# Attention and ternary FFN on one core: the FFN's middle layer laid out with its channels on partitions

## The chip, the cores and the metric

The kernel runs on one core of a Trainium2 chip. Its engines work side by side, each through its own queue in order: TensorE (PE, with its weight loads as PEld), VectorE (DVE), ScalarE (ACT), GpSimd (POOL) and SyncE (SP, which here only starts DMAs). The metric is the device time of one execution, in microseconds; lower is better. The kernel before takes 735.78 us (median of three runs, 735.1 to 738.06).

## The reference

The input x is 8 x 1024 x 256 in float32. First comes a linear attention with 16 heads of 16, its own LayerNorm and an output projection, added to x, and a LayerNorm. Then comes a feed-forward network, added to its input, and a last LayerNorm:

```python
h = layer_norm(x, ln1_g, ln1_b)
h = jnp.einsum('bsd,hd->bsh', h, ternary_quant(w1)) + b1     # 256 -> 1024
h = jax.nn.gelu(h, approximate=False)
h = layer_norm(h, ln2_g, ln2_b)                              # over the 1024
out = jnp.einsum('bsh,dh->bsd', h, ternary_quant(w2)) + b2   # 1024 -> 256
```

`ternary_quant` turns a weight matrix into -1, 0 and 1 times one scale. The middle layer is what lies between the two products: bias, gelu, and a LayerNorm over its 1024 channels.

## The kernel before

The 8192 rows are 16 blocks of 512 rows (`blocks`), a block being four tiles (`G`) of 128 rows; x stays in SBUF (`xs`) all the time and takes the results in place. The program is written out by hand in one order (`manual_schedule`), and each engine gets its instructions in that order. The main loop runs 18 times (`i`): for i up to 15 it makes the keys, queries and state of block i, and it does `attend` for block i - 2. Small DVE work of the attention's LayerNorms waits in the lists `soon` and `later` and is dealt out a few steps at a time by `more(n)`; the normalised rows are written by ACT through `apply(n)`. The weights' quantisation (`prepare1`, `prepare2`) is dealt out the same way, by `next(prep)`.

The FFN is a generator, `ffn_slots`, of one slot for each of 128 chunks (16 blocks times 8). Its slots are drawn 13 times in the last two turns of the main loop (`slot()`, i = 16 and 17), where the last two blocks are attended, and then one after the other to the end, with `more(8)` and `apply(2)` after each. In the code:

- `enter` (L571): POOL multiplies a block's rows by a scale into `h0` (L576), and a POOL DMA adds the row `bout` onto x (L579).
- `turn_input` (L583): PE turns `h0`, ACT and DVE split it into two fp32r halves `hT`, high and low (`halves`, L568 on ACT and L569 on DVE). A value goes through the fp32r products as these two halves.
- `hidden` (L597), once a slot: 128 rows by 512 channels. The rows are the stationary operand and `t1` moves: four products of 512 columns (L615), and a fifth of a row of ones with the row `brow`, which adds the bias (L619). ACT applies Gelu and sums along the row (L620).
- `squares` (L629), every second slot: ACT squares the deviation from the mean over 1024 channels, with the sum taken along (L632).
- `turn` (L636), once a slot: four transposes bring 128 channels of the block's 512 rows onto partitions (L643), then the halves `u`, scaled by ln2's gain (L568, L569).
- `product` (L648), once a slot: eight products of 256 columns (L657) add the chunk to the outputs `pf` of four row tiles, which sit two to a PSUM bank.
- `norms` and `outputs`, in fixed slots of a block: DVE computes the two inverse roots with integer steps and three Newton steps (`rsqrt`, L122 to L131), adds the mean term (`add_mean`, L680), adds the product out of PSUM to x (L716), takes statistics (L686, L687); `finish` (L663) lets POOL write the last LayerNorm (L670) and SP store the block (L673).

A slot s works on `product(s)`, `turn(s + 2)` and `hidden(s + 11)`: `hidden` runs 11 slots ahead.

Of the kernel before, what the change touches and what calls it, by code (L numbers as in the profile page):

```python
# [22 lines left out]
def attn_ffn_postln_kernel(  # L23
# [29 lines left out]


# [4 lines left out]
    t2 = const.tile([P, HC, C], F32R, name="t2")  # L59
# [6 lines left out]
    bkv = const.tile([P, 2 * KC], F32, name="bkv")  # L66
    nc.sync.dma_start(xs[0][:, 0:G, :], x0[:, 0:G, :])
    nc.scalar.dma_start(wqkv_sb[:, :, C : 2 * C], w3[:, :, C : 2 * C])
    with nc.allow_non_contiguous_dma("two vectors of 256"):
        nc.gpsimd.dma_start(bkv, rows[C : 3 * C].rearrange("(i p) -> p i", p=P))  # L70
# [9 lines left out]
    )  # L80
    for b in range(1, B):
        nc.sync.dma_start(xs[b], x[b].rearrange("(p t) c -> p t c", p=P))
# [10 lines left out]
    nc.vector.memset(ones, 1.0)  # L93

# [42 lines left out]
    brow = const.tile([P, HID], F32R, name="brow")  # L137
    ones_r = const.tile([P, P], F32R, name="ones_r")
    g2sum = const.tile([P, C], F32, name="g2sum")
    bout = const.tile([P, C], F32, name="bout")  # L140
    nc.vector.memset(ones_r.bitcast(F32), 1.0)
# [3 lines left out]
    def quantise(w, t_sb, inv, name):  # L145
        t_all = t_sb.rearrange("p a b -> p (a b)")
        n = t_all.shape[1]
        o = min(w.shape[1], 512)

        def pieces(what):  # L150

            for k in range(w.shape[0] // P):
                for c in range(0, w.shape[1], o):
                    piece = big.tile([P, TB], F32, tag="hA", bufs=4, name=f"{what}_{name}_{k}_{c}")
                    nc.sync.dma_start(piece[:, :o], w[k * P : (k + 1) * P, c : c + o])
                    yield k * w.shape[1] + c, piece[:, :o]
# [10 lines left out]
        for i, piece in ahead(pieces("wm")):  # L167
            yield
            nc.vector.tensor_reduce(
                part[:, i // o : i // o + 1], piece, AX.X, ALU.add, apply_absolute_value=True  # L170
            )
# [4 lines left out]
        total = ps.tile([P, TB], F32, tag="tp", bufs=2, name=f"total_{name}")  # L176
# [6 lines left out]
        for i, piece in ahead(pieces("wq")):  # L183
            yield
            nc.vector.tensor_scalar(piece, piece, scale, 1.0, ALU.mult, ALU.min)
            nc.vector.tensor_scalar(piece, piece, -1.0, ROUND, ALU.max, ALU.add)
            nc.vector.tensor_scalar(t_all[:, i : i + o], piece, ROUND, None, ALU.subtract)

    def spread(made, cols, vec, name):

        if not made:
            made.append(big.tile([P, HC, P], F32, tag="h0", bufs=2, name=f"col_{name}"))
        for j in cols:
            nc.vector.tensor_scalar(made[0][:, j, :], ones, vec[:, j : j + 1], None, ALU.mult)
        return made[0]

    def prepare1():
# [4 lines left out]
        sel = const.tile([P, 1], F32, name="sel")  # L202
        nc.vector.tensor_tensor(sel, ident[:, 0:1], ident[:, 1:2], ALU.subtract)
        for j in range(0, HID, 512):
            yield
            b1_b = big.tile([P, TB], F32, tag="hA", bufs=4, name=f"b1_{j}")
            nc.sync.dma_start(
                b1_b, rows[5 * C + j : 5 * C + j + TB].partition_broadcast(P)
            )
            col = spread([], range(KC), ln1_b, f"1_{j}")  # L210
            yield
            pb = ps.tile([P, TB], F32, tag="tp", bufs=2, name=f"pb_{j}")
            for k in range(KC):
                nc.tensor.matmul(
                    pb, col[:, k, :], t1[:, k, j : j + 512].bitcast(F32),
                    start=(k == 0), stop=(k == KC - 1),
                )
            full = b1_b
            nc.vector.scalar_tensor_tensor(full, pb, inv1, b1_b, ALU.mult, ALU.add)
            yield  # L220
            hi = big.tile([P, TB], F32R, tag="hA", bufs=4, name=f"hi_{j}")
            nc.vector.tensor_copy(hi, full)

            nc.vector.tensor_scalar(full, full, ident[:, 1:2], None, ALU.mult)
            nc.vector.scalar_tensor_tensor(
                brow[:, j : j + 512], hi.bitcast(F32), sel, full, ALU.mult, ALU.add
            )

    def prepare2():

        yield from quantise(w2, t2, inv2, "w2")
        for i, vec in enumerate((ln2_g, ln2_b)):
            made = []
            for j in range(0, HC, 2):
                yield
                col = spread(made, (j, j + 1), vec, f"2_{i}")
            yield
            pg = ps.tile([P, TB], F32, tag="tp", bufs=2, name=f"ps2_{i}")
            for j in range(HC):
                nc.tensor.matmul(  # L240
                    pg[:, 0:C], col[:, j, :], t2[:, j, :].bitcast(F32),
                    start=(j == 0), stop=(j == HC - 1),
                )
            if i == 0:
                nc.vector.tensor_copy(g2sum, pg[:, 0:C])
            else:
                nc.vector.scalar_tensor_tensor(bout, pg[:, 0:C], inv2, b2_b, ALU.mult, ALU.add)
# [11 lines left out]
    def prepare0():  # L259
        yield  # L260
        col = spread([], range(KC), ln_b, "0")
        pc = ps.tile([P, TB], F32, tag="tp", bufs=2, name="ps_crow")
        for k in range(KC):
            nc.tensor.matmul(
                pc[:, 0:C], col[:, k, :], wo_sb[:, k, :], start=(k == 0), stop=(k == KC - 1)
            )
        nc.vector.tensor_tensor(crow, pc[:, 0:C], bo_b, ALU.add)
        yield
        pm = ps.tile([P, TB], F32, tag="tp", bufs=2, name="ps_mean")
# [27 lines left out]
    def turned(dst, src, k, name):  # L297

        pt = ps.tile([P, TB], F32, tag="tp", bufs=2, name=name)
# [44 lines left out]
    def turn_keys(i, t):  # L344
# [3 lines left out]
        pt = ps.tile([P, TB], F32, tag="tp", bufs=2, name=f"pte_{i}_{t}")  # L348
# [97 lines left out]
    def state_turn(b):  # L446
        pt = ps.tile([P, TB], F32, tag="tp", bufs=2, name=f"pta_{b}")
# [9 lines left out]
    def state_values(b):  # L457

        pst = ps.tile([P, TB], F32, tag="tp", bufs=2, name=f"pst_{b}")
# [14 lines left out]
    def state_out(b, c):  # L474
# [3 lines left out]
        pm = ps.tile([P, TB], F32, tag="tp", bufs=2, name=f"psm_{b}_{c}")  # L478
# [7 lines left out]
    def attend(i, t):  # L486
# [6 lines left out]
        if t == 0:  # L493
            ys[i] = big.tile([P, G, C], F32, tag="y", bufs=5, name=f"y_{i}")
# [7 lines left out]
        o = big.tile([P, KC, P], F32, tag="o", bufs=4, name=f"o_{i}_{t}")  # L502
# [59 lines left out]
    SLOTS = len(blocks) * HC  # L562
    LEAD = HC + 3
    h0, hT, h, u, pf, mv, rs, sc, ms = {}, {}, {}, {}, {}, {}, {}, {}, {}

    def halves(hi, lo, src, gain):

        nc.scalar.activation(hi, src, AF.Copy, scale=gain)  # L568
        nc.vector.scalar_tensor_tensor(lo, src, gain, hi.bitcast(F32), ALU.mult, ALU.subtract)  # L569
# [13 lines left out]
    def turn_input(i, k):  # L583
        if k == 0:
            tag, bufs = ("xT", 2) if i % 2 == 0 else ("qT", 3)
            hT[i] = [
                big.tile([P, KC, TB], F32R, tag=tag, bufs=bufs, name=f"hT_{i}_{s}")
                for s in range(2)
            ]
        pt = ps.tile([P, TB], F32, tag="tp", bufs=2, name=f"pth_{i}_{k}")  # L590
# [4 lines left out]
        halves(hT[i][0][:, k, :], hT[i][1][:, k, :], pt, gs1[:, k : k + 1])  # L595

    def hidden(m):  # L597


        i, t, half = m // HC, m % HC // 2, m % 2  # L600
        if half == 0:
            if t == 0:
                h[i] = []

                mv[i] = small.tile([P, 2 * G, 2], F32, tag="mvh", name=f"mvh_{i}")
                if i == 0:
                    nc.vector.memset(mv[i][:, :G, :], 1.0)
            tag, bufs = ("hA", 4) if i % 2 == 0 else ("y", 5)
            h[i].append(big.tile([P, HID], F32, tag=tag, bufs=bufs, name=f"h_{i}_{t}"))
            h[i, t] = small.tile([P, 2], F32, tag="total", name=f"total_{i}_{t}")  # L610
        cols_j = slice(half * 512, (half + 1) * 512)
        ph = ps.tile([P, TB], F32, tag="w", bufs=4, name=f"ph_{m}")
        for s in range(2):
            for k in range(KC):
                nc.tensor.matmul(  # L615
                    ph, hT[i][s][:, k, t * P : (t + 1) * P], t1[:, k, cols_j],
                    start=(s == 0 and k == 0), stop=False,
                )
        nc.tensor.matmul(ph, ones_r, brow[:, cols_j], start=False, stop=True)  # L619
        nc.scalar.activation(  # L620
            h[i][t][:, cols_j], ph, AF.Gelu, accum_out=h[i, t][:, half : half + 1]
        )
        if half == 1:
            nc.vector.tensor_scalar(  # L624
                mv[i][:, G + t, 0:1], h[i, t][:, 0:1], h[i, t][:, 1:2], -1.0 / HID,
                ALU.add, ALU.mult,
            )

    def squares(i, t):  # L629

        sq = big.tile([P, HID], F32, tag="sq", name=f"sq_{i}_{t}")
        nc.scalar.activation(  # L632
            sq, h[i][t], AF.Square, bias=mv[i][:, G + t, 0:1], accum_out=mv[i][:, G + t, 1:2]
        )

    def turn(s):  # L636

        i, j = s // HC, s % HC
        tag, bufs = (("q", 2), ("ekT", 1), ("q", 2), ("ek", 1))[s % 4]
        u[s] = big.tile([P, 2, TB], F32R, tag=tag, bufs=bufs, name=f"u_{s}")  # L640
# [275 lines left out]
```

## Time and profile before

| what | value |
|---|---|
| three runs, median | 735.78 us |
| the profiled execution, its own time | 737.86 us |
| its span, first to last instruction | 736.2 us |
| mean granted TensorE clock | 0.981 |
| busy PE / PEld / DVE / ACT / POOL | 690.2 / 548.9 / 556.3 / 441.6 / 177.0 us |
| first `hidden` product (L615) starts | 351.5 us |
| first `product` (L657) starts | 379.9 us |
| last `product` starts | 723.9 us |
| last store is issued | 732.6 us |

The span has three parts: attention to about 351 us, a mixture of the last two attended blocks and the first FFN slots to 380 us, and FFN alone from there. A row of a group of instructions gives line, engine, operation, output and inputs with their shapes, how often, total busy time, the mean of one, then the engine's idle time just before them and what ended it. A row of the timeline gives start, duration, engine, line, operation and how many like it are merged. The duration of one instruction holds its latency, and instructions of one engine overlap (eight L657 of 0.28 us each span 1.20 us in the timeline), so what an engine spends on each is read from the distance between two starts.

### The profile page before, as it was taken

Reading aid. Unit: us, or ns where it says so; the run is one execution under the profiler, and the core shown is the slowest. Engines: PE = TensorE matmul, PEld = TensorE weight load, DVE = VectorE, ACT = ScalarE, POOL = GpSimd, SP = SyncE. Lnnn points to the kernel's source line nnn. Section 1 sums busy time; section 2 is a strip of 40 time slices with the busy share of each in tenths; the row PEclk is TensorE's granted clock in tenths of the full one; section 3 lists DMA queues with packets and bytes.
Section 4 is the critical chain, followed back from the end, with each engine's and each line's share of the span. In section 5 each row is a group of like instructions: output and inputs, shape, how many; then the busy total and the mean of one; then the engine's idle time right before and its main releaser. Section 6 shows DMA issues by size and latency. Waiting matters only on the chain.

```text
span 736.2 us, 10803 instructions
## 1 busy us (share of the span) xinstructions
PE 690.2 (94%) x3780; PEld 548.9 (75%) x3780; DVE 556.3 (76%) x1642; ACT 441.6 (60%) x970; POOL 177.0 (24%) x156
## 2 busy tenths in 40 slices
PE   6899999979989999997998899999999999999992
PEld 4677766757657777765776788888888888888882
DVE  1567799886997859797888766767766777776686
ACT  2245445635464545646797677677677677776760
POOL 1222213121221212224310023333113333113112
PEclk9999999998999999999999999999999999999998
DMA  9832203222011211203510022220122220222001
GB/s 329 292 86 48 40 15 65 51 44 51 8 30 28 30 29 18 40 1 57 87 29 1 1 58 58 58 57 31 29 58 58 58 57 30 30 57 58 30 30 58
DMA packets 25687, 40.43 MB, mean 55 GB/s; under 512 B 1600, under 2 KB 21056, under 8 KB 24736
## 3 DMA queue, kind: packets, MB, share of 16 engines
q0 software_dynamic: 17056, 17.17, 15.8%
q1 hardware_dynamic: 7344, 21.50, 7.8%
q10 hardware_dynamic: 1232, 1.06, 0.4%
q8 instruction: 30, 0.49, 0.3%
q14 instruction: 25, 0.20, 0.1%
HBM read 14.56 MB, written 8.39 MB: 31 GB/s over the span
## 4 chain that ended last, share of the span: by engine, by line
PE 63%; DVE 19%; issue 9%; ACT 4%; DMA 3%; POOL 2%; ACTq 0%; POOLq 0%; DVEq 0%
PE ph L615 12%; PE pf L657 12%; PE po L498 7%; PE pt L643 5%; PE pa L407 5%; PE pq L364 5%; PE pk L322 5%; PE ph L619 3%; DMA wo_sb<-in_wo_dram 3%; DVE x L526 2%; DVE st_y L532 2%; POOL x L670 2%; PE ptq L301 1%; PE pth L592 1%; PE ptx L301 1%
## 5 line engine op out<-in xcount | busy, mean ns | idle before, releaser
L657 PE MATMUL pf<-t,u 128*128 128x256 f32 x1024 | 156.8, 294 | 4.0 <-DVE x L716 3.6
L569 DVE SCALAR_TENSOR_TENSOR u<-pt,cols_sb,u 128x512 fp32r<-128x512 f32 x128 | 95.6, 747 | 66.0 <-ACT u L568 64.3
L615 PE MATMUL ph<-t,hT 128*128 128x512 f32 x512 | 143.7, 402 | 0.0
L657 PEld LDWEIGHTS pf<-t,u 128*128 128x128 f32 x1024 | 131.0, 189 | 10.0 <-issue 5.8
L620 ACT ACTIVATE h<-ph 128x512 f32<-128x512 f32 x128 | 76.6, 598 | 84.6 <-PE ph L619 74.3
L670 POOL TENSOR_SCALAR x<-x,ny_f,sh 128x256 f32<-128x256 f32 x60 | 38.5, 652 | 270.9 <-DVE sh L667 270.9
L615 PEld LDWEIGHTS ph<-t,hT 128*128 128x128 f32 x512 | 88.7, 189 | 13.6
L498 PE MATMUL po<-sm,qT 128*128 128x384 f32 x256 | 96.6, 502 | 0.0
L568 ACT ACTIVATE u<-pt,cols_sb 128x512 fp32r<-128x512 f32 x128 | 87.5, 684 | 8.4 <-PE pt L643 8.4
L643 PE MATMUL pt<-ident,h 128*128 128x128 f32 x512 | 77.8, 274 | 4.7 <-DVE u L569 2.6
L643 PEld LDWEIGHTS pt<-ident,h 128*128 128x128 f32 x512 | 61.3, 140 | 21.2 <-DVE hT L569 7.0
L632 ACT ACTIVATE sq<-h,mvh 128x1024 f32<-128x1024 f32 x64 | 73.8, 1153 | 1.9 <-DVE mvh L624 1.9
L378 POOL TENSOR_TENSOR q<-q,qm 128x1024 f32<-128x1024 f32 x16 | 30.8, 1926 | 149.8 <-DVE qm L377 90.5
L407 PE MATMUL pa<-x,ek 128*128 128x256 f32 x256 | 63.2, 392 | 0.0
L364 PE MATMUL pq<-wqkv_sb,xT 128*128 128x256 f32 x256 | 60.6, 380 | 1.0 <-DMA wqkv_sb<-in_wqkv_dram 1.0
L322 PE MATMUL pk<-xT,wqkv_sb 128*128 128x512 f32 x128 | 60.9, 599 | 0.0
L407 PEld LDWEIGHTS pa<-x,ek 128*128 128x128 f32 x256 | 50.5, 198 | 13.5 <-issue 0.6
L498 PEld LDWEIGHTS po<-sm,qT 128*128 128x128 f32 x256 | 45.8, 195 | 18.8 <-issue 1.7
L364 PEld LDWEIGHTS pq<-wqkv_sb,xT 128*128 128x128 f32 x256 | 47.9, 190 | 12.8 <-issue 3.1
L391 POOL TENSOR_TENSOR q<-q,rq 128x1024 f32<-128x1024 f32 x16 | 31.0, 1935 | 108.8 <-DVE rq L390 63.1
L338 ACT ACTIVATE ekT<-pk,nb 128x512 f32<-128x512 f32 x32 | 21.7, 683 | 55.3 <-DVE nb L335 29.5
L619 PE MATMUL ph<-brow,ones_r 128*128 128x512 f32 x128 | 50.7, 396 | 0.0
(144 smaller groups left out, 1109.9 us busy)
## 6 DMA issues: line engine op xcount, KB each, us to landing
x<-crow POOLq DMA_DIRECT2D x16, 512.0 KB, 5.5
x<-bout POOLq DMA_DIRECT2D x16, 512.0 KB, 5.5
out_dram<-x SPq DMA_DIRECT2D x16, 512.0 KB, 2.6
x<-in_x_dram SPq DMA_DIRECT2D x7, 1024.0 KB, 9.8
x<-in_x_dram SPq DMA_DIRECT2D x2, 512.0 KB, 5.8
wm_w<-in_w_dram SPq DMA_DIRECT2D x4, 256.0 KB, 4.0
wq_w<-in_w_dram SPq DMA_DIRECT2D x4, 256.0 KB, 2.5
wm_w<-in_w_dram SPq DMA_DIRECT2D x8, 128.0 KB, 2.1
```

Source lines behind the costliest of these rows:

```text
L322: nc.tensor.matmul(pk, wqkv_sb[:, k, C + c * P : C + (c + 1) * P], xT[i][:, k, :], start=(k == 0), stop=(k == KC - 1),)
L364: nc.tensor.matmul(pq[:, n, :], xT[i][:, k, (t + n) * P : (t + n + 1) * P], wqkv_sb[:, k, 0:C], start=(k == 0), stop=(k == KC - 1),)
L407: nc.tensor.matmul(pa[i][:, c, :], ek[i][:, t, c * P : (c + 1) * P], x_of(i)[:, t, :], start=(t == 0), stop=(t == G - 1),)
L498: nc.tensor.matmul(po[:, c * P : c * P + P + C], qT[i][:, c, t * P : (t + 1) * P], sm[b][:, c, :], start=(c == 0), stop=(c == KC - 1), ski ...
L568: nc.scalar.activation(hi, src, AF.Copy, scale=gain)
L569: nc.vector.scalar_tensor_tensor(lo, src, gain, hi.bitcast(F32), ALU.mult, ALU.subtract)
L615: nc.tensor.matmul(ph, hT[i][s][:, k, t * P : (t + 1) * P], t1[:, k, cols_j], start=(s == 0 and k == 0), stop=False,)
L619: nc.tensor.matmul(ph, ones_r, brow[:, cols_j], start=False, stop=True)
L620: nc.scalar.activation(h[i][t][:, cols_j], ph, AF.Gelu, accum_out=h[i, t][:, half : half + 1])
L632: nc.scalar.activation(sq, h[i][t], AF.Square, bias=mv[i][:, G + t, 0:1], accum_out=mv[i][:, G + t, 1:2])
L643: nc.tensor.transpose(pt[:, t * P : (t + 1) * P], h[i][t][:, j * P : (j + 1) * P], ident)
L657: nc.tensor.matmul(pf[i][t // 2][:, t % 2, :], u[s][:, n, t * P : (t + 1) * P], t2[:, j, :], start=(j == 0 and t % 2 == 0 and n == 0), sto ...
```

## The change

The middle layer is made with channels on partitions. A chunk is now 128 channels by the block's 512 rows. `hidden` takes `t1` as the stationary operand and moves `hT`: four products of 512 columns into a bank `ph`. The bias is a column now, so Gelu takes it as its per-partition operand (`bh`), in place in PSUM. ACT copies `ph` to the high half of `u`, scaled by `gm`, and squares `ph` about a constant `shift` into `sq`; DVE makes the low half (`lower`). The transposes of `turn`, the bias products, the row sums and `spread` are gone.

The sum of squares over channels is now a sum over partitions: POOL adds the eight `sq` of a block into `sums` (seven adds of 128 x 512), and four small products with a column of ones (`sum_squares`) make it a number per row. The row sums of h come from two more columns of `t2` (258 instead of 256), which hold the high and low half of 1/`gm`; `gm` is the gain's mantissa, and its power of two goes into `t2`. `shift` is minus the mean of gelu(bias) over all channels; `scales` corrects the variance for it.

`pf` is one bank for each of the four row tiles (tag `w`); at a block's end ACT copies them to SBUF (`take`, into `z`), and DVE's `output` reads `z`. `ph` rotates through three banks (two of tag `o`, one `tq`), `u` through nine buffers (`RING`). The inverse root of the FFN's scales (`power`) is a POOL power with one Newton step; the two other roots keep `rsqrt`.

The order of a block is the string `ORDER`: P is a product, H a `hidden` with its ACT work, r a portion (`R`) of the previous block's closing DVE work (`rest`), e an `enter`, a and b the two `turn_input`, s `sum_squares`. H runs seven to eight chunks ahead of P. In this stage `more` deals one step every second unit and `apply` one every eighth; in the turns 16 and 17 of the main loop they are cut to two and one. `prep` ends one turn earlier, and the first `enter` and `turn_input` go into turns 13 and 14. Some attention buffers shrink (`y` from 5 to 4, `o` from 4 to 3), the PSUM tag `tp` becomes two tags in turn, and the bias comes by one more POOL DMA at the start.

```diff
...
-    t2 = const.tile([P, HC, C], F32R, name="t2")
+
+    t2 = const.tile([P, HC, C + 2], F32R, name="t2")
...
+    with nc.allow_non_contiguous_dma("vectors of 512 and 1024"):
+        nc.gpsimd.dma_start(b1, rows[5 * C :].rearrange("(i p) -> p i", p=P))
...
+        yield
+        pb = ps.tile([P, TB], F32, tag=next(turning), bufs=1, name="pb1")
+        for j in range(HC):
             for k in range(KC):
                 nc.tensor.matmul(
-                    pb, col[:, k, :], t1[:, k, j : j + 512].bitcast(F32),
-                    start=(k == 0), stop=(k == KC - 1),
+                    pb[:, j : j + 1], t1[:, k, j * P : (j + 1) * P].bitcast(F32),
+                    ln1_b[:, k : k + 1], start=(j == 0 and k == 0),
+                    stop=(j == HC - 1 and k == KC - 1), skip_group_check=True,
                 )
+        nc.vector.scalar_tensor_tensor(bh, pb[:, 0:HC], inv1, b1, ALU.mult, ALU.add)
...
+        yield
+        gb = cols_sb[:, 8:24].rearrange("p (v j) -> p v j", v=2)
+        pg = yield from rows_of(
+            lambda j: t2[:, j, :C].bitcast(F32), lambda j: gb[:, :, j], HC, "2"
+        )
+        nc.vector.tensor_copy(g2sum, pg[:, 0, :])
+        nc.vector.scalar_tensor_tensor(bout, pg[:, 1, :], inv2, b2_b, ALU.mult, ALU.add)
+        yield
...
+        nc.vector.tensor_scalar(
+            gm.bitcast(I32), ln2_g.bitcast(I32), 0x7FFFFF, 0x3F800000,
+            ALU.bitwise_and, ALU.bitwise_or,
+        )
...
+        nc.vector.reciprocal(inv, gm)
+        nc.vector.tensor_copy(t2[:, :, C], inv)
+        nc.vector.tensor_tensor(t2[:, :, C + 1], inv, t2[:, :, C].bitcast(F32), ALU.subtract)
+        for j in range(HC):
...
+            nc.vector.tensor_scalar(
+                t2[:, j, :C], t2[:, j, :C].bitcast(F32), power[:, j : j + 1], None, ALU.mult
+            )
...
-            ys[i] = big.tile([P, G, C], F32, tag="y", bufs=5, name=f"y_{i}")
+            ys[i] = big.tile([P, G, C], F32, tag="y", bufs=4, name=f"y_{i}")
...
-        o = big.tile([P, KC, P], F32, tag="o", bufs=4, name=f"o_{i}_{t}")
+        o = big.tile([P, KC, P], F32, tag="o", bufs=3, name=f"o_{i}_{t}")
...
+    WEIGHT = 8
+    ORDER = "ePHaPHPrHrPbHPrHrPrHrsPrHrPrHr"
+    RING = (("xT", 2), ("xT", 2), ("ekT", 1), ("ek", 1), ("q", 2), ("q", 2), ("qT", 3), ("qT", 3), ("qT", 3))
...
-                for s in range(2)
+                big.tile([P, KC, TB], F32R, tag="hA", bufs=4, name=f"hT_{i}_{n}") for n in range(2)
...
+    def hidden(n):
+
+        i, j = n // HC, n % HC
+        tag, bufs = ("w", 4) if n < 6 else (("o", 2), ("o", 2), ("tq", 1))[n % 3]
+        ph[n] = ps.tile([P, TB], F32, tag=tag, bufs=bufs, name=f"ph_{n}")
         for s in range(2):
             for k in range(KC):
                 nc.tensor.matmul(
-                    ph, hT[i][s][:, k, t * P : (t + 1) * P], t1[:, k, cols_j],
+                    ph[n], t1[:, k, j * P : (j + 1) * P], hT[i][s][:, k, :],
+                    start=(s == 0 and k == 0), stop=(s == 1 and k == KC - 1),
                 )
-        nc.tensor.matmul(ph, ones_r, brow[:, cols_j], start=False, stop=True)
-        nc.scalar.activation(
-            h[i][t][:, cols_j], ph, AF.Gelu, accum_out=h[i, t][:, half : half + 1]
-        )
+        nc.scalar.activation(ph[n], ph[n], AF.Gelu, bias=bh[:, j : j + 1])
+        tag, bufs = RING[n % len(RING)]
+        u[n] = big.tile([P, 2, TB], F32R, tag=tag, bufs=bufs, name=f"u_{n}")
+        nc.scalar.activation(u[n][:, 0, :], ph[n], AF.Copy, scale=gm[:, j : j + 1])
+
+    def lower(n):
+
+        j = n % HC
+        nc.vector.scalar_tensor_tensor(
+            u[n][:, 1, :], ph[n], gm[:, j : j + 1], u[n][:, 0, :].bitcast(F32),
+            ALU.mult, ALU.subtract,
+        )
+
+    def squares(n):
+
+        i, j = n // HC, n % HC
+        sq[n] = big.tile([P, TB], F32, tag="sq", bufs=3, name=f"sq_{n}")
+        nc.scalar.activation(sq[n], ph[n], AF.Square, bias=shift)
+        if j == 1:
+            sums[i] = big.tile([P, TB], F32, tag="sums", bufs=2, name=f"sums_{i}")
+        if j > 0:
+            first = sq[n - 1] if j == 1 else sums[i]
+            nc.gpsimd.tensor_tensor(sums[i], first, sq[n], ALU.add)
+
+    def sum_squares(i):
+
+        pq = ps.tile([P, TB], F32, tag="tp", bufs=1, name=f"psq_{i}")
         for t in range(G):
-            nc.tensor.transpose(
-                pt[:, t * P : (t + 1) * P], h[i][t][:, j * P : (j + 1) * P], ident
-            )
-        halves(u[s][:, 0, :], u[s][:, 1, :], pt, ln2_g[:, j : j + 1])
-
-    def product(s):
-
-        i, j = s // HC, s % HC
+            nc.tensor.matmul(
+                pq[:, t : t + 1], sums[i][:, t * P : (t + 1) * P], ones[:, 0:1],
+                start=(t == 0), stop=(t == G - 1), skip_group_check=True,
+            )
+        sn[i] = small.tile([P, G], F32, tag="sn", name=f"sn_{i}")
+        nc.vector.tensor_scalar(sn[i], pq[:, 0:G], 1.0 / HID, EPS, ALU.mult, ALU.add)
...
+                ps.tile([P, C + 2], F32, tag="w", bufs=4, name=f"pf_{i}_{t}") for t in range(G)
...
+                    pf[i][t], u[n][:, s, t * P : (t + 1) * P], t2[:, j, :],
+                    start=(j == 0 and s == 0), stop=(j == HC - 1 and s == 1),
                 )
...
+    def take(i, t):
+
+        if t == 0:
+            zs[i] = big.tile([P, G, C + 2], F32, tag="z", bufs=1, name=f"z_{i}")
+        nc.scalar.copy(zs[i][:, t, :], pf[i][t])
...
+        nc.gpsimd.tensor_tensor(y, v, mhalf[:, :n], ALU.pow)
+        yield 20
+        nc.vector.tensor_tensor(t, y, y, ALU.mult)
+        yield
+        nc.vector.scalar_tensor_tensor(t, t, -0.5, v, ALU.mult, ALU.mult)
+        yield
+        nc.vector.scalar_tensor_tensor(y, t, 1.5, y, ALU.add, ALU.mult)
+        return y
...
+        nc.vector.tensor_scalar(v[:, :G], mv[i - 1][:, :, 1], EPS, None, ALU.add)
...
+        nc.vector.tensor_reduce(total, zs[i][:, :, C : C + 2], AX.X, ALU.add)
...
+        nc.vector.tensor_scalar(dev, total, 1.0 / HID, shift, ALU.mult, ALU.add)
...
+        nc.vector.scalar_tensor_tensor(dev, dev, -1.0, dev, ALU.mult, ALU.mult)
...
+        nc.vector.tensor_tensor(v[:, G:], sn[i], dev, ALU.add)
...
+        nc.vector.tensor_scalar(v[:, G:], v[:, G:], EPS, None, ALU.max)
...
+        rs[i] = yield from power(v, f"f_{i}")
...
+        nc.vector.tensor_scalar(sc[i], rs[i][:, G:], inv2, None, ALU.mult)
...
+        nc.vector.scalar_tensor_tensor(ms[i], total, -1.0 / HID, sc[i], ALU.mult, ALU.mult)
...
+    def output(i, t):
+        x_t = x_of(i)[:, t, :]
+        nc.vector.scalar_tensor_tensor(
+            x_t, zs[i][:, t, :C], sc[i][:, t : t + 1], x_t, ALU.mult, ALU.add
+        )
...
+        def H():
+            for n in made:
+                hidden(n)
+                squares(n)
+                L()
+                low.append(n)
+                break
+
+        def R():
+
+            weight = 0
+            while after and weight < WEIGHT:
+                step = next(after[0], None)
+                if step is None:
+                    after.pop(0)
+                else:
+                    weight += step
+
+        def rest(i):
+
+            for weight in scales(i):
+                yield weight or 2
             if i > 0:
-                finish(i - 1, mv[i][:, :G, 0], rs[i][:, :G])
-            sc[i] = small.tile([P, G], F32, tag="sc", name=f"sc_{i}")
-            nc.vector.tensor_scalar(sc[i], rs[i][:, G:], inv2, None, ALU.mult)
+                finish(i - 1, rs[i][:, :G])
+            for step, weight in ((output, 4), (add_mean, 4), (result_stats, 5)):
+                for t in range(G):
+                    step(i, t)
+                    yield weight
+
         enter(0)
+        enter(1)
         yield
         turn_input(0, 0)
+        yield
         turn_input(0, 1)
-        for s in range(-LEAD, SLOTS):
+        yield
+        nc.scalar.activation(held, bh, AF.Gelu, accum_out=one)
+        yield
+        pk = ps.tile([P, TB], F32, tag="tp", bufs=1, name="pshift")
+        nc.tensor.matmul(pk[:, 0:1], ones, one, start=True, stop=True)
+        nc.vector.tensor_scalar(shift, pk[:, 0:1], -1.0 / HID, None, ALU.mult)
+        for n in range(7):
+            H()
             yield
+            if n in (3, 5):
+                turn_input(1, (n - 3) // 2)
+            L()
+        enter(2)
+        for i in range(len(blocks)):
+            p = iter(range(i * HC, (i + 1) * HC))
+            for what in ORDER:
+                if what == "P":
+                    n = next(p)
+                    product(n)
+                    L()
+                    if n % HC == HC - 1:
+                        while after:
+                            R()
+                        for t in range(G):
+                            take(i, t)
+                        after.append(rest(i))
+                elif what == "H":
+                    H()
+                elif what == "r":
+                    R()
+                    continue
+                elif what == "e" and i + 3 < len(blocks):
+                    enter(i + 3)
+                elif what in "ab" and i + 2 < len(blocks):
+                    turn_input(i + 2, "ab".index(what))
+                elif what == "s":
+                    sum_squares(i)
+                yield
+        while after:
+            R()
...
-        for _ in range(n):
+        for _ in range(2 if ffn else n):
...
-        for _ in range(n):
+        for _ in range(1 if ffn else n):
...
+        slot(i == len(blocks) - 2)
...
+            slot(i == len(blocks) - 2)
...
+        slot(i == len(blocks) - 1)
...
-        if i == len(blocks) - 2:
+        if i == len(blocks) - 3:
...
-    for _ in slots:
-        more(8)
-        apply(2)
+    for n, _ in enumerate(slots):
+        if n % 2 == 0:
+            more(1)
+        if n % 8 == 0:
+            apply(1)
...
```

## The prediction

> **What bounds the kernel now.** I read the busy times first, then stage windows, then the timeline of a few slots where FFN runs alone, then single rows.
>
> ```profile
> PE 690.2 (94%) x3780; PEld 548.9 (75%) x3780; DVE 556.3 (76%) x1642; ACT 441.6 (60%) x970; POOL 177.0 (24%) x156
> ```
>
> The windows below give, for each stretch, its length and the busy time of PE, PEld, DVE, ACT and POOL, then the granted clock. In the last row PE is busy 309.94 of 313 us; DVE and ACT have some 27% to spare.
>
> ```profile
> 351.00:380.00 29.00, 29.00 (x135) 21.59 (x133) 24.41 (x93) 24.65 (x62) 7.94 (x6) 1.00 0.45 66
> 380.00:411.00 31.00, 25.42 (x158) 21.53 (x157) 27.83 (x107) 22.67 (x51) 0.00 (x0) 0.96 0.00 1
> 411.00:724.00 313.00, 309.94 (x2061) 271.73 (x2060) 228.27 (x676) 221.24 (x472) 76.50 (x84) 1.00 0.20 45
> ```
>
> The timeline of slots in that stage; read the distances between starts.
>
> ```profile
> 560.10 0.60 PE L643 MATMUL pt<-ident,h 128*128 128x128 f32 x4
> 560.45 1.20 PE L657 MATMUL pf<-t,u 128*128 128x256 f32 x8
> ...
> 565.91 0.60 ACT L620 ACTIVATE h<-ph 128x512 f32<-128x512 f32 x1 [1.80 <-PE ph L619]
> 566.07 1.20 PE L657 MATMUL pf<-t,u 128*128 128x256 f32 x8
> 566.41 0.19 ACT L620 ACTIVATION_READ_ACCUMULATOR h<-ph 128x1 f32 x1
> 566.50 0.68 ACT L568 ACTIVATE u<-pt,cols_sb 128x512 fp32r<-128x512 f32 x1
> ...
> 567.07 1.16 ACT L632 ACTIVATE sq<-h,mvh 128x1024 f32<-128x1024 f32 x1
> 567.10 1.10 PE L615 MATMUL ph<-t,hT 128*128 128x512 f32 x4
> ...
> 568.04 0.39 PE L619 MATMUL ph<-brow,ones_r 128*128 128x512 f32 x1
> ...
> 568.27 0.60 PE L592 MATMUL pth<-ident,h 128*128 128x128 f32 x4
> ```
>
> On PE four transposes take 0.35 (560.10 to 560.45), eight `product` matmuls 1.03, four `hidden` ones 0.94, the bias one 0.23: 2.55 us a slot. A `turn_input` is 0.43 (568.27 to the next group at 568.70), two a block. A block is 8 x 2.55 + 0.86 = 21.26; measured, the `product` groups at 453.72 and 651.21 in the chain lie nine blocks apart, 21.94 each. So 0.68 a block is waiting. PE is the bound, by its own work.
>
> **PE after.** Gone per chunk: 0.35 of transposes and 0.23 of bias. Two more columns on 256 add 1%, 0.01. Left: 1.98 + 0.11 of `turn_input`. `sum_squares` is four f32 products, two passes each (L177 shows x4 for two calls): eight weight loads at about 0.12 apart (L657's are 0.13), 1.0 a block, 0.12 a chunk. Together 2.20 a chunk, 17.6 a block, 4.3 less than the 21.94.
>
> **ACT after.** A 512-column pass with a per-partition operand hands over after 0.57 (566.50 to 567.07). Gelu, copy and square make 1.71, which is what the old slot paid too (Gelu 0.59 with its accumulator, copy 0.57, half a square 0.57). But the copy reads what Gelu wrote in place. No row of before shows such an ACT pair; DVE's L686 and L687, of which the second needs the first, start 0.45 apart at a duration of 0.42, so I take Gelu's full 0.68 + 0.03 for the first: 1.85. The ends are 1.71, and 2.13 if all three wait so. `turn_input` adds 0.14, `take` 4 x 0.27 a block (L504's distance to the next), 0.14. In all 2.13 a chunk, 17.0 a block.
>
> **DVE after**, per block: ten low halves at 0.66 (L569 at 570.43, next start 571.09): 6.6. `output` 4 x 0.42 and `add_mean` 4 x 0.43 (two L680 in 0.87): 3.4. Statistics 4 x 0.55: 2.2. About thirteen small steps at 0.20 (L122 to L131 start 0.20 apart): 2.6. Sum 14.8; the old block had 16 (228.27 of 313, times 21.94).
>
> The attention's last norms are also DVE's: `more` is cut to two a call, so of some 130 steps (52 for batch 6, twice 39 for batch 7; 16 tiles x 1.0 + 6 roots x 2.2 + small ones = 31 us) only about 24 run in turns 16 and 17. The other 106, 25 us, go one in two units, 20 units a block, so they last 10.6 blocks and cost 2.4 us in each. Before, they filled the window from 380 to 411.
>
> **POOL and DVE.** The new load on POOL is seven adds of 512 a block at half of L391's 1.93, 0.96 each, beside `enter` (1.9), its DMA (1.3) and `finish` (2.2). This is what speaks against the change:
>
> ```profile
> 327.76 1.93 POOL L391 TENSOR_TENSOR q<-q,rq 128x1024 f32<-128x1024 f32 x1 [9.09 <-DVE rq L390]
> ...
> 328.04 0.40 DVE L532 BATCH_NORM_STATS2 st_y<-x 128x6 f32<-128x256 f32 x1
> ...
> 328.69 1.04 DVE L539 TENSOR_SCALAR nvy<-mvy 128x8 f32<-128x8 f32 x1
> ```
>
> ```profile
> L526 DVE SCALAR_TENSOR_TENSOR x<-y,ny_o,x x64: 450/453/1833, 95.1 to 403.3; 128x256 f32<-128x256 f32 x64
> ```
>
> L539, an eight-element step of 0.16 us, ended only with POOL's 1.93 us op; L526 (two SBUF inputs) went from 0.45 to 1.83 us six times, each time under L378 on POOL. Statistics, and steps with one input in PSUM such as L569, run through. `output` loses that freedom: it read PSUM (L716), now it reads `z`. Ends: 0, if each add lies under a low half; 8.6 a block, if DVE sits out every add and `enter`. I take 2.0: an add and its low half are freed together by the square, so 0.96 - 0.66 = 0.3 is left, in the five chunks with portions `r`, and 0.5 for `enter`.
>
> The Trainium skill (SBUF — State Buffer, Who interferes with whom) calls this an exclusive lock for the whole instruction, for a two-input DVE op against any POOL op that reads SBUF; L526 agrees. L680 under L670, a one-input POOL op, doesn't quite: 0.48 in the median and 0.76 at most, against 0.56 for a full L670. By the page `finish` could cost DVE 2.2 a block more, 33 us over the stage and a total near 733; by the row 0.3 a block.
>
> The POOL power: no row. Ends 0.34 (L102, a small POOL op) and 1.93 (a 1024-wide one); I take 1.0, as it has 8 elements. It stands on POOL behind an add, and DVE's next Newton step behind it, with all later `lower` queued after that; a low half of 0.66 covers part: 0.7 lost a block (0 to 2).
>
> So DVE is 14.8 + 2.0 + 0.7 = 17.5 a block, and 19.9 while norms remain.
>
> **Waits.** `ph` has three banks: filling 0.94, ACT 1.85, `lower` 0.66 and hand-overs, under 4.5 us, against three chunks' time of 6.9; a late `lower` by up to 2.4 stops nobody. `pf` has no second set: the first product of a block waits for four `take` on ACT behind the square of the last H. PE has one H to fill in; 0.5 a block, about the old loss at L716, which goes.
>
> No row shows ACT and DVE reading one bank together. The Trainium skill (PSUM — Partial Sum Buffer, PSUM bank collisions raise a hardware error) says they must not, so `lower` would follow the square; I have it so above, and the sum stays either way.
>
> **The sum**, against the profiled execution (span 736.2 and 1.66 around it, 737.86, which is 2.1 over the median).
> - To 380: unchanged. In turns 16 and 17 PE does some 6 us less (nine H for twelve), ACT 1.4 more on 24.65 of 29, and `po` must share its banks with `ph`: between -4 and +4. Preparations: `spread` (8.4 us of DVE) and two products (L214, L240, 11 us of PE) leave, some 7 us of small PE passes come: 0 to -3. The bias DMA issues in twice L70's 0.93 ahead of `ident`, which then is ready at 6.0 where PE waited for x until 5.77: 0.2.
> - Then 119 H remain. Early blocks go at DVE's 19.9, 2.50 a chunk with 0.1 of waits: 85 x 2.50 = 212. Late ones at PE's 17.6 + 0.8 of waits, 2.30: 34 x 2.30 = 78. Seven products alone at 1.05: 7.4.
> - The end. Before, 12 us from the last product to the end. Now `take` 1.4, six small steps 1.2, power 1.2, five steps 0.9, `output`, `add_mean` and statistics 5.5, then as before from the last variance on (727.7 to 736.2) 8.5, and 2 because the rest of block 14 is longer than the last eight products: 21.
>
> 380 + 297 + 21 + 1.7 = 700; less 2 for the median, 698. I say 699.
>
> **The rivals.**
> - *PE stays the bound in all blocks* (adds always hidden, norms absorbed): 18.3 x 14.9 + 7.4 = 280, in all 681. DVE's spare time before speaks for it, the moved norms against it. 0.17.
> - *ACT becomes the bound*: all three passes wait for each other, 2.13 + 0.28 = 2.41 and waits make 2.50 a chunk everywhere: 119 x 2.50 = 298, in all 706. 0.15.
> - *The gain is eaten*: DVE loses 2 us a block more than I took: 727 to 735. 0.08.
> - *Slower: POOL's adds lock out DVE.* Where DVE reaches its two-input steps just as each add begins, it waits, `lower` behind it comes late, `ph` isn't freed and PE stops. Equal time is reached at (737.9 - 1.7 - 380 - 7.4 - 21) / 14.9 = 22.0 a block; my blocks average 19.6, so it decides from 2.4 us a block more, of the 6.6 still possible. At half of these: 23, 749. L526's six waits speak for it; that bn_stats and low halves run beneath the adds speaks against it. 0.10.
>
> Forecast: 0.50 for 686 to 718. The range, 677 to 730, leaves out half the slow rival, part of the eaten gain and the very best. 0.5%, 3.7 us, is about what a measurement of this kernel tells from no change: faster 0.85, same 0.05, slower 0.10.
>
> **What would show it.** Right: L643 and L619 without successors; `product` and `hidden` groups 1.03 and 0.94 apart; three ACT passes in about 1.85; PE idle in early blocks behind `lower`, DVE over 90% busy there, late blocks 1.5 us shorter; two-input DVE steps stretched by up to 0.96. Wrong: a copy starting far later than 0.71 after Gelu, a power of several us, PE waiting for `take` by more than 1 us a block, or granted clock under 1.0 in the FFN because PE pauses (it fell to 0.84 from 405 to 410, with PE busy half the time).

## The result: slower, 758.4 us for 736.9

The changed kernel takes 758.44 us in the median of four runs (753.08 to 760.87), beside 736.92 (735.1 to 739.28) for the kernel before on the same chip. The ratio is 1.028, 95% interval 1.0216 to 1.0344. I had forecast 699, and 677 to 730 as the range. The profiled execution has a span of 751.4 us, 753.1 with what lies around it.

The busy times of the changed kernel:

```profile
PE 653.7 (87%) x3284; PEld 518.3 (69%) x3284; DVE 620.1 (83%) x1518; ACT 461.8 (61%) x908; POOL 354.0 (47%) x285
```

PE lost 496 instructions and 36.5 us, as meant. DVE executes 124 instructions fewer than before and is busy 64 us longer. POOL's busy time doubled. The windows of the changed kernel, with the columns of the windows before (length, busy time of PE, PEld, DVE, ACT and POOL, granted clock, DMA):

```profile
351.00:380.00 29.00, 24.24 (x107) 17.21 (x106) 19.67 (x45) 23.89 (x48) 14.67 (x11) 0.94 0.20 29
380.00:411.00 31.00, 26.50 (x168) 23.25 (x166) 25.91 (x57) 25.63 (x45) 18.60 (x14) 0.97 0.24 35
411.00:729.00 318.00, 278.91 (x1558) 246.45 (x1559) 296.13 (x632) 238.01 (x420) 218.09 (x185) 0.87 0.18 41
```

In the last row DVE is busy 93% of the time; before it was 73%. PE went from 309.94 of 313 us at clock 1.00 to 278.91 of 318 at clock 0.87. The FFN stage didn't become shorter at all. One block takes 22.85 us on average (the copies into `z` of thirteen blocks lie 297.0 us apart), where it took 21.94.

A timeline of the changed kernel shows what keeps DVE "busy". These are some lines of DVE, POOL and PE around 577:

```profile
576.97 1.34 POOL L589 DMA_DIRECT2D x<-bout  x1 [0.64 <-POOL h L586]
577.00 0.23 DVE L714 TENSOR_SCALAR sc<-ny_f,inv 128x4 f32<-128x4 f32 x1
577.27 3.61 DVE L717 SCALAR_TENSOR_TENSOR ms<-total,sc 128x4 f32<-128x4 f32 x1
...
577.84 1.79 POOL L643 TENSOR_TENSOR sums<-sums,sq 128x512 f32<-128x512 f32 x1
...
579.10 1.75 POOL L643 TENSOR_TENSOR sums<-sq,sq 128x512 f32<-128x512 f32 x1
...
580.81 0.15 DVE L741 SCALAR_TENSOR_TENSOR sh<-mvf,ny_f 128x4 f32<-128x4 f32 x1
...
581.67 0.74 DVE L629 SCALAR_TENSOR_TENSOR u<-ph,gm,u 128x512 fp32r<-128x512 f32 x1
...
582.46 1.00 PE L617 MATMUL ph<-hT,t 128*128 128x512 f32 x3 [2.50 <-DVE u L629]
```

L717 has two inputs in SBUF and four columns. It needs 0.16 us. Here it stands for 3.61, until POOL has finished its DMA (the second half of `enter`) and two adds that had piled up behind `enter`. `lower` (L629) is queued behind it on DVE, so `ph` isn't freed and PE stands 2.5 us.

I summed such holds for every DVE instruction from 380 us on: its duration less the lower quartile of those of the same line and shapes that no POOL instruction overlaps. Before, they come to 7.4 us; in the changed kernel to 99.6. Sixteen blocks close in that time, so that is 6.2 us a block. Twelve steps stand over 2 us (2.7 to 3.8), one for each `enter` of this stage, and each ends at most 0.3 us after the second of two adds that follow `enter`'s DMA without a gap.

### The profile page after: what moved, and what is told of

Read it like the earlier page. It is cut to its first block, busy times and chain, and to the rows that moved or that the text cites. A ratio compares the mean times of both kernels' runs of the same rounds, so it can differ in the third digit from the quotient of the medians.

```text
span 751.4 us, 9897 instructions
## 1 busy us (share of the span) xinstructions
PE 653.7 (87%) x3284; PEld 518.3 (69%) x3284; DVE 620.1 (83%) x1518; ACT 461.8 (61%) x908; POOL 354.0 (47%) x285
## 4 chain that ended last, share of the span: by engine, by line
DVE 43%; PE 34%; ACT 12%; issue 5%; DMA 3%; POOL 2%; ACTq 0%; POOLq 0%
PE po L511 7%; DVE u L629 6%; PE pq L377 5%; PE pk L335 5%; PE pa L420 5%; DVE x L721 4%; ACT sq L638 4%; DVE x L728 3%; PE ph L617 3%; ACT ph L621 3%; DVE x L539 3%; DMA wo_sb<-in_wo_dram 3%; PE pf L665 2%; DVE hT L606 2%; DVE st_y L545 2%
## 5 line engine op out<-in xcount | busy, mean ns | idle before, releaser
L617 PE MATMUL ph<-hT,t 128*128 128x512 f32 x512 | 161.7, 442 | 40.5 <-DVE u L629 40.2
L643 POOL TENSOR_TENSOR sums<-sums,sq 128x512 f32<-128x512 f32 x96 | 132.6, 1381 | 91.5 <-ACT sq L638 89.5
L665 PE MATMUL pf<-t,u 128*128 128x258 f32 x1024 | 161.5, 305 | 4.8 <-ACT z L674 2.9
L665 PEld LDWEIGHTS pf<-t,u 128*128 128x128 f32 x1024 | 152.2, 208 | 18.4 <-ACT z L674 7.5
L617 PEld LDWEIGHTS ph<-hT,t 128*128 128x128 f32 x512 | 97.5, 210 | 59.8 <-DVE u L629 45.4
L621 ACT ACTIVATE ph<-ph,bh 128x512 f32<-128x512 f32 x128 | 85.4, 667 | 74.6 <-PE ph L617 72.4
L629 DVE SCALAR_TENSOR_TENSOR u<-ph,gm,u 128x512 fp32r<-128x512 f32 x128 | 94.6, 741 | 11.5 <-ACT sq L638 11.2
L624 ACT ACTIVATE u<-ph,gm 128x512 fp32r<-128x512 f32 x128 | 88.1, 688 | 4.1
L638 ACT ACTIVATE sq<-ph,shift 128x512 f32<-128x512 f32 x128 | 87.1, 681 | 2.7 <-POOL sums L643 2.5
L721 DVE SCALAR_TENSOR_TENSOR x<-z,sc,x 128x256 f32<-128x256 f32 x64 | 49.5, 817 | 0.0
L539 DVE SCALAR_TENSOR_TENSOR x<-y,ny_o,x 128x256 f32<-128x256 f32 x64 | 47.9, 748 | 0.2
```

What stands on the lines that cost most here:

```text
L617: nc.tensor.matmul(ph[n], t1[:, k, j * P : (j + 1) * P], hT[i][s][:, k, :], start=(s == 0 and k == 0), stop=(s == 1 and k == KC - 1),)
L621: nc.scalar.activation(ph[n], ph[n], AF.Gelu, bias=bh[:, j : j + 1])
L624: nc.scalar.activation(u[n][:, 0, :], ph[n], AF.Copy, scale=gm[:, j : j + 1])
L629: nc.vector.scalar_tensor_tensor(u[n][:, 1, :], ph[n], gm[:, j : j + 1], u[n][:, 0, :].bitcast(F32), ALU.mult, ALU.subtract,)
L638: nc.scalar.activation(sq[n], ph[n], AF.Square, bias=shift)
L643: nc.gpsimd.tensor_tensor(sums[i], first, sq[n], ALU.add)
```

## The experiments

The first four runs stood beside runs of the kernel before with a median of 737.36, the last three beside 737.09. The "holds" of each kernel are the sum just described.

**One add for seven** (six of the eight squares are left out of the variance):

```diff
-        if j > 0:
-            first = sq[n - 1] if j == 1 else sums[i]
-            nc.gpsimd.tensor_tensor(sums[i], first, sq[n], ALU.add)
+        if j == 1:
+            nc.gpsimd.tensor_tensor(sums[i], sq[n - 1], sq[n], ALU.add)
```

> The changed kernel with one POOL add a block instead of seven; six of eight squares are left out of the variance. Lock theory (POOL's two-input adds keep DVE's two-input steps waiting, low halves come late behind them, PE pauses and its clock falls as a consequence): the waits of DVE's steps, about 100 us over the FFN in the changed kernel or 6.4 a block, fall below 30; blocks go from 23 to 25 us to 18.5 to 19.5; granted clock in the FFN back to 0.97 or more; time 690 to 708. Load theory (DVE simply has too much to do, with the attention's last norms on top, and PE pauses for that): DVE's work is unchanged, time stays at 740 or more. Power theory (the POOL power of 1.66 us, which the Newton steps wait for, is what holds DVE up): power and its place stay, so at most a third of the loss goes, time 740 to 750.

Measured: 690.22 us, ratio 0.936 (0.932 to 0.9396); holds 24.9 us. Blocks are 17.9 to 20.5 at first and 17.6 to 17.7 later, and the stage has its clock back:

```profile
411.00:660.00 249.00, 234.44 (x1500) 206.71 (x1499) 218.57 (x614) 234.72 (x420) 106.65 (x100) 1.00 0.23 52
```

Without six adds that no DVE step takes as an input, 68 us go, though DVE executes the same 1518 instructions. In the changed kernel, all waits of ACT and PE for the sums come to only 4.6 us, so the adds are the cause, and they act through DVE. The rest of the change works about as forecast.

**The roots on DVE** instead of POOL's power:

```diff
-        rs[i] = yield from power(v, f"f_{i}")
+        rs[i] = yield from rsqrt(v, f"f_{i}")
```

> The changed kernel with the FFN's inverse roots by DVE's integer start and three Newton steps, as before the change, instead of a POOL power and one step. Power theory: 16 times 1.66 us on POOL and the wait behind it go, time 725 to 740. Lock theory: POOL is shorter by 1.66 a block, but DVE gets eight more small steps, all of a kind that waits for an add, so little moves: 748 to 770.

Measured: 775.85 us, ratio 1.0524 (1.0487 to 1.0561); holds 87.3. Some 17 us slower than with the power, a little beyond what the lock theory allowed. The power isn't what costs the time. The holds are 12 us fewer, but DVE executes 128 more steps, and PE's waits for `lower` grow from 40.2 to 61.0 us. That the longer queue on DVE makes them grow is argued, not shown.

**The adds on DVE**, which computes all that the reference does:

```diff
-            nc.gpsimd.tensor_tensor(sums[i], first, sq[n], ALU.add)
+            nc.vector.tensor_tensor(sums[i], first, sq[n], ALU.add)
```

> The changed kernel with the seven adds of a block on DVE instead of POOL; same result. Lock theory: DVE gets 7 x 0.6 = 4.2 us a block more, but loses some 5 of its 6.4 us of waits; about the same or a little faster than the changed kernel, 735 to 758, with the clock up and DVE still the bound. Load theory: DVE at 83% of the span gets 67 us more and nothing back, time 790 to 820.

Measured: 710.57 us, ratio 0.9634 (0.9595 to 0.9673); holds 10.3. It is faster than I expected and beats the kernel before. The groups of L643 in this kernel and in the changed one, with busy time and mean duration:

```profile
L643 DVE TENSOR_TENSOR sums<-sums,sq 128x512 f32<-128x512 f32 x96 | 66.1, 688 | 5.7 <-ACT sq L638 5.7
```

```profile
L643 POOL TENSOR_TENSOR sums<-sums,sq 128x512 f32<-128x512 f32 x96 | 132.6, 1381 | 91.5 <-ACT sq L638 89.5
```

DVE makes an add in half of POOL's time. Seven of them cost DVE 7 x 0.688 = 4.8 us a block; with POOL making them, holds cost it 6.2, of which 0.6 remain here. From 380 us to the last product DVE is busy 292.9 us for 322.2 in the changed kernel and idle 12.9 for 27.0, at a granted clock of 0.99 for 0.88. Blocks are near 22.4 while the attention's norms remain and then 18.2 to 18.4, and DVE sets the pace:

```profile
411.00:660.00 249.00, 228.34 (x1424) 198.73 (x1423) 243.31 (x674) 225.32 (x399) 91.22 (x84) 0.99 0.24 52
```

`enter` and its DMA are still on POOL. The step L717, which stood 3.61 us above, now runs at its own length in the middle of that DMA, so the DMA by itself doesn't hold it:

```profile
576.04 1.34 POOL L589 DMA_DIRECT2D x<-bout  x1 [0.30 <-POOL h L586]
...
576.95 0.15 DVE L717 SCALAR_TENSOR_TENSOR ms<-total,sc 128x4 f32<-128x4 f32 x1
```

**The sum of squares on PE**: a product with a matrix of ones per chunk, eight gathered in one PSUM bank, its row copied by ACT; the squares are then rounded for the fast product, and the block 0 keeps POOL's adds. `pth` had to give up its bank and shares one with `ph`.

```diff
+        nc.tensor.matmul(psq[i], ones_r, sq[n], start=(j == 0), stop=(j == HC - 1))
...
-        pt = ps.tile([P, TB], F32, tag="tp", bufs=1, name=f"pth_{i}_{k}")
+        pt = ps.tile([P, TB], F32, tag="tq", bufs=1, name=f"pth_{i}_{k}")
```

> The changed kernel with the squares added up by PE: one fp32r product a chunk of a block of ones with the squares (512 columns), gathered in a PSUM bank over eight chunks, copied out as a row by ACT and turned by four small products into free columns of the output's bank; only block 0 keeps POOL's adds. The squares are rounded to fp32r. Lock theory: PE gets 8 x 0.235 = 1.9 us a block more, DVE's waits fall below 30 us in all, blocks of 18.5 to 20, clock 0.97 or more, time 692 to 712, under the kernel before. Load theory: nothing goes from DVE and PE gets more, time 758 or above.

Measured: 787.81 us, ratio 1.0689 (1.0647 to 1.0731), a miss. The holds are gone (8.9), and yet it is the slowest. Its waits (total, times, longest) say what came instead:

```profile
DVE u L632 <- ACT sq L641: 121.7, 85, 4.2
...
ACT ph L624 <- PE ph L620: 82.2, 65, 4.2
...
PE pth L604 <- DVE u L632: 27.2, 12, 4.2
```

The last line is the shared bank: `pth` cannot be filled before `lower` has read the `ph` that lies there. PE takes its work in order, so the next `hidden` waits too, ACT waits for that and DVE for ACT. This chain is my reading of the waits; no run takes the shared bank away. The run doesn't tell against the lock, since this kernel changed more than the place of the adds. What a PE sum with banks of its own would give stays open.

**`enter`'s multiply on ACT**, the adds left on POOL:

```diff
-        nc.gpsimd.tensor_tensor(
-            h0[i], x_of(i), rs2.unsqueeze(2).to_broadcast([P, G, C]), ALU.mult
-        )
+        for t in range(G):
+            nc.scalar.activation(
+                h0[i][:, t, :], x_of(i)[:, t, :], AF.Copy, scale=rs2[:, t : t + 1]
+            )
```

> The changed kernel with enter's multiply (1.9 us on POOL, once a block until block 15) made by ACT in four passes of 256; its DMA and all seven adds stay on POOL. If what holds DVE longest is the row enter, its DMA, add without a gap on POOL (single DVE steps of 3.3 to 3.8 us once a block), some 2 to 2.5 us a block go in thirteen blocks: 758 - 26 to 33 = 725 to 732, and blocks near 22. If the adds do it by themselves, little moves: 748 to 757. ACT pays 1.4 a block more; if ACT's queue were the bound, 760 to 775.

Measured: 732.35 us, ratio 0.9935 (0.991 to 0.996), 26 us better than the changed kernel, as the row of `enter`, DMA and adds would have it. The four-element step (minimum, median and maximum in ns), in the changed kernel, then here, then with one add and `enter` back on POOL:

```profile
L717 DVE SCALAR_TENSOR_TENSOR ms<-total,sc x16: 161/164/3657, 410.1 to 736.8; 128x4 f32<-128x4 f32 x16
```

```profile
L718 DVE SCALAR_TENSOR_TENSOR ms<-total,sc x16: 161/164/1280, 408.1 to 716.1; 128x4 f32<-128x4 f32 x16
```

```profile
L716 DVE SCALAR_TENSOR_TENSOR ms<-total,sc x16: 161/164/165, 409.3 to 674.9; 128x4 f32<-128x4 f32 x16
```

`enter` with one add holds this step not at all, seven adds without `enter`'s multiply hold it for one add (1.28), and both together for 3.66. Other steps are held a little longer, up to 1.72 with one add and 1.94 here, but never for two adds. The holds add up to 77.6, 22 less than in the changed kernel; the two profiled executions lie 20.7 apart. So the sum of the holds fell by about as much as the time, and that a long hold costs more than short ones of the same sum isn't shown. What changed for PE is the length of its waits. Those of `hidden` for `lower`, first in the changed kernel, then here:

```profile
PE ph L617 <- DVE u L629: 40.2, 22, 4.9
```

```profile
PE ph L618 <- DVE u L630: 37.7, 29, 2.8
```

The total is about the same, the longest is not: 9 waits of 22 were over 2.4 us, here it is 1 of 29. After the long ones PE starts again at half speed; the products of the changed kernel after one such wait:

```profile
411.80 2.07 PE L617 MATMUL ph<-hT,t 128*128 128x512 f32 x4 [4.86 <-DVE u L629]
413.68 1.70 PE L649 MATMUL psq<-ones,sums 128*128 128x1 f32 x8
415.24 2.07 PE L665 MATMUL pf<-t,u 128*128 128x258 f32 x8
417.10 1.91 PE L617 MATMUL ph<-hT,t 128*128 128x512 f32 x4
```

and the window around it, in the changed kernel and then with `enter` on ACT:

```profile
410.00:420.00 10.00, 8.20 (x32) 7.43 (x33) 9.76 (x30) 2.85 (x5) 1.27 (x1) 0.53 0.01 2
```

```profile
410.00:420.00 10.00, 8.19 (x42) 7.09 (x43) 9.86 (x20) 7.29 (x15) 4.88 (x4) 0.83 0.01 2
```

PE is busy equally long and gets 42 instructions done where it got 32. From 380 us to the last product PE is busy 305.6 us in the changed kernel and 287.6 here, for nearly the same work, at a mean clock of 0.88 and 0.96. How the 26 us divide between holds and clock I did not measure separately; no run changes one without the other.

**Both: adds on DVE, `enter`'s multiply on ACT** (the two edits above together).

> The changed kernel with the seven adds on DVE (710.6 by itself) and also enter's multiply on ACT. What is left of the lock from 380 on is 11 us there, of which about half lies under enter: 700 to 708. DVE is busy 39 of 40 us in that kernel, so it is its own work that bounds it: if enter cost DVE nothing, 708 to 713.

Measured: 707.2 us, ratio 0.9574 (0.9524 to 0.9624); holds 5.6. That overlaps the interval of adds on DVE alone, so where no adds are on POOL `enter` costs about 3 us or nothing, for 26 with them. The early blocks gained a little and the late ones went from 18.3 to 19.0, and ACT, which now makes the multiply, is busy 18.5 us of such a block; with the adds alone moved it is 17.2. No engine has much left in the 249 us from 411 to 660: ACT 236.3, DVE 236.4, PE 227.6.

**Two adds of seven back on POOL**, the rest as in the run before:

```diff
-            nc.gpsimd.tensor_tensor(sums[i], first, sq[n], ALU.add)
+            eng = nc.gpsimd if j in (2, 7) else nc.vector
+            eng.tensor_tensor(sums[i], first, sq[n], ALU.add)
```

> As the run before, with two of the seven adds (of chunks 2 and 7 of a block, whose slots have few closing steps of DVE beside them) back on POOL, five on DVE. DVE saves 2 x 0.68 = 1.4 us a block: in sixteen blocks up to 22 us, 680 to 698, if an add on POOL costs DVE nothing where DVE has only low halves to make. If each POOL add still holds DVE for its 1.28 us, the saving turns into a loss of 2 x 0.6 a block: 715 to 728.

Measured: 717.84 us, ratio 0.9731 (0.9684 to 0.9778); holds 30.2. DVE saves 2 x 0.69 x 16 = 22 us of adds and loses 25 more in holds. So even an add placed in a slot with little beside it costs DVE a little more than making it. That balance is 3 us; the time rose by 10.6, and where the rest comes from isn't shown.

## Why the prediction was wrong

- **The lock: the step that failed.** I had its mechanism, its rows and both ends (0 to 8.6 us a block), and took 2.0. Measured are 6.2. I let an add of 0.96 start with a low half of 0.66 and counted the 0.3 left over. Two things were wrong in that. A low half, with one input in PSUM, does run beneath an add (never over 0.753 us), but while the add still runs a step usually follows that it does hold: 83 of the stage's 105 adds lie over a held step. And I priced each add by itself, where they pile up: `enter` and its DMA take POOL for 3.2 us, two adds then follow without a gap, and a waiting DVE step gets in only behind both.
- **POOL's add** takes 1.30 in the median where POOL was free before it, and I took half of a 1024-wide one, 0.96.
- **The slower rival** (POOL's adds lock out DVE, 0.10, 749 us, from 2.4 us a block over my 2.0) is what happened: 4.2 over it. With its condition the sum by my own terms would have come to 380 + 14.9 x 23.8 + 7.4 + 21 + 1.7 = 765, for 753 in the profile. L526's six waits, which I had named as speaking for it, came in a kernel with 156 POOL instructions; the changed one has 285.
- **A late `lower` stops nobody up to 2.4 us.** I failed to use this bound: the twelve holds of 2.7 to 3.8 pass it. Nor do the runs show that it is right: with `enter` on ACT no hold passes 1.94, and PE still waits 29 times for `lower`, 37.7 us in all. PE's pauses then brought the clock to 0.87, which I had named as a sign of being wrong but not priced.
- **PE's work, 17.6 a block,** was right: 17.5 with one add (234.44 of 249, at 18.6 a block).
- **ACT's passes, 1.85 a chunk,** were right. In the changed kernel their starts lie 0.69, 0.59 and 0.57 apart:

```profile
571.32 0.66 ACT L621 ACTIVATE ph<-ph,bh 128x512 f32<-128x512 f32 x1
...
572.01 0.69 ACT L624 ACTIVATE u<-ph,gm 128x512 fp32r<-128x512 f32 x1
...
572.60 0.68 ACT L638 ACTIVATE sq<-ph,shift 128x512 f32<-128x512 f32 x1
...
573.17 0.69 ACT L605 ACTIVATE hT<-pth,gs 128x512 fp32r<-128x512 f32 x1
```

- **DVE's own work, 14.8 a block,** was too high: with the adds on DVE a late block of 18.3 has 18.0 of DVE work, of which 4.8 are adds, so 13.2. The norms end after five or six blocks, not 10.6, and cost about 4 in each, not 2.4.
- **The power** takes 1.66, not 1.0, inside its ends. Replacing it made the kernel slower.
- **The wait for `take`** is small: 10.4 us in 20 waits of PE and its loads. **Start and tail** were right: eight `hidden` are done at 380, so 120 remain where I had 119, and from the last product (729) to the end it is 22 for 21. From 380 to 729 it is 349 where I had 297; that 52 is nearly the whole error of the profiled execution (753.1 for 700).
- **`finish` under the two readings.** The row said 0.3 a block, though its 0.76 came under `enter`; under `finish` alone L680 took 0.69 at most. With the adds on DVE, `output` beside `finish` is never over 0.65 us, so the row was right. The Trainium skill (SBUF — State Buffer, Who interferes with whom) would let such a one-input POOL op block DVE's two-input steps for its whole length; these runs don't show that. What it says of two-input DVE steps against POOL is what the adds did.

## What to carry to other kernels

Work given to POOL isn't free because POOL is idle: price it by what DVE does meanwhile. Here, with DVE busy 93% of the stage (the holds included), an elementwise add on POOL cost DVE 0.8 to 0.9 us in holds (89 us for the 105 adds of the stage, 25 for 30 in the last run), and DVE made it in 0.69. Before two POOL operations are put next to each other, look for what may queue behind them, since a DVE step waited for the whole row; and look at the longest hold as well as the sum, with the time that the buffers cover.

## What the hardware showed that I had not expected

- A DVE step of four columns stood 3.61 us, across a POOL DMA's end and two adds: POOL's next operations went ahead of a DVE step that was already waiting. With `enter`'s multiply off POOL it was never over 1.28. In its row the step begins 0.57 us before the first add's; why it is held already then isn't shown, since the same DMA without adds behind it held nothing.
- Steps with one tensor input are held as well: `sc` (L714), a multiply of four columns by a per-partition scalar, takes 0.23 us and stood up to 3.77. Such steps carry 12 of the 99.6 us.
- POOL's add shows up to 1.84 us where it follows another POOL operation without a gap. Its row then begins up to 0.5 us before that operation's end; counted from that end it takes 1.24 in the median, no longer than alone (1.30). So these rows don't show DVE holding POOL.
- A POOL power of 8 columns takes 1.66 us, more than an add of 512.
- After a pause of 4.9 us PE ran at half clock for over 7 us: from 411 to 419 the granted clock is 0.50, with PE busy 7.2 of the 8 us. The Trainium skill (TensorE: Matmul & The Clock Gate, Part 1) says that a pause brings half rate, and that some 3.4 us of sustained work end it; here it took about twice that.
